# Graph network node update: both layers in one step, and a last update of 384 columns

## The chip, the core and the metric

The kernel runs on one core of a Trainium2 chip. The metric is the device time of one execution, in microseconds (us), as the median of several runs. The engines of the core are named as the profile names them: PE is TensorE (PEld its weight loads), DVE is VectorE, ACT is ScalarE, POOL is GpSimd, and SP issues most of the transfers.

## What is computed

There are 12500 nodes with 64 features and 200000 edges with 32 features; edges are sorted by destination. Each edge makes a message, messages are summed at the destination, and the node is updated, added to itself and normalized:

```python
msg_in = jnp.concatenate([nodes[row], nodes[col], edge_features], axis=-1)
messages = _mlp(msg_in, mW1, mb1, mW2, mb2)          # relu(x @ W1 + b1) @ W2 + b2
aggregated = jax.ops.segment_sum(messages, col, num_segments=nodes.shape[0])
upd_in = jnp.concatenate([nodes, aggregated], axis=-1)
x = _layernorm(x + _mlp(upd_in, uW1, ub1, uW2, ub2), axis=-1)
```

`row` is the source, `col` the destination. The hidden layers have 128 features.

## The kernel before

The product with the source's features is made once per node: a table A (L414 to L422) holds x @ W1 for the source part, a table B (L424 to L430) that for the destination part with the bias. Per edge, only rows of these tables are added.

The edges are cut into 1563 tiles of 128. A step of the main loop (L583) deals with one subgroup of 6 tiles (NSUB = 261 subgroups, the last of 3 tiles); two subgroups make a group of 12. For each tile POOL gathers 128 rows of A by an indirect DMA (L168); the gathered rows of a subgroup are one buffer of a pool with 18 (ROWB). The first 10 subgroups gather rows of x instead. All gathers are issued by POOL in order, as far ahead as buffers allow (L585).

In step s the loop does this, in this order on each engine:

- `norm` of an update (L358): on DVE a reciprocal and the scaling of each block of 128 nodes.
- `windows(s + 2)` (L217): SP loads 32 rows of B per tile (L229).
- `node_part(s)` (L260): DVE adds the gathered rows to the products in PSUM (L276), ACT applies relu (L277); this gives h.
- `collect(s - 1)` (L287): PE adds h into the sums of the open update by a selection matrix (L302), and counts edges (L307). The products transpose the result: 128 features by up to 480 node columns.
- `close` (L318): when the last subgroup of an update has been collected, ACT copies sums and counts to SBUF (L321, L322).
- every second step `select`, `load` and `counts` (L187 to L215): the selection matrices of the next group.
- `edge_part(s + 1)` (L246): PE makes the edge and destination products of the next subgroup in PSUM (L256).
- `carry` (L310): the sums of nodes that lie in both updates go over to the next one (L315, L316).
- `update` (L333): the first layer of the node update on PE, 448 columns (L337, L338), and its relu on ACT (L339, tile hTu).
- `residual` (L341): the second layer plus x on PE, for 4 blocks of 128 nodes (L346, L347), the statistics on DVE (L351, L353) and the square root on ACT (L355).
- `columns` (L326): SP loads the columns of x for an update (L330).
- `store` (L368): SP writes a finished update (L370).

Updates are not evenly spaced. A destination number is drawn as a square, so later edges hold more nodes; `updates()` (L51) places 33 of them, the first after 47 subgroups and the last ones every 4. `due` (L575) gives the step in which an update's first layer runs. Update 31 is due in step 258 and update 32, the last, in step 262; the loop runs to step 264. In the version before, the first layer runs in step `due` behind `edge_part`, the second layer in the step after it, norm and store in the one after that:

```python
            if s + 1 < NSUB:
                edge_part(s + 1)
            if s in due and due[s] + 1 < K:
                carry(due[s] + 1)
            if s in due:
                update(due[s])
            if s - 1 in due:
                residual(due[s - 1])
```

The order is written out by hand (manual_schedule): each engine runs its instructions in the order of these calls. The PSUM tiles pc (products), pu (first layer) and py (second layer) share two buffers; a new tile takes the one that was released first, and waits for its last reader.

After the loop a flag is read (L623); a branch for unusual inputs (L625) is not taken.

Of the kernel before, what the change touches and what calls it, by code (L numbers as in the profile page):

```python
# [10 lines left out]
F32 = mybir.dt.float32  # L11
I32 = mybir.dt.int32
AF = mybir.ActivationFunctionType
ALU = mybir.AluOpType
# [3 lines left out]
P = 128  # L18
N, D, DE, DH = 12500, 64, 32, 128
E = 200000  # L20
# [4 lines left out]
SUB = 6  # L25
# [5 lines left out]
WIN = 32  # L31
# [12 lines left out]
UB = 4  # L44
NCOL = (-(-N // P) + UB) * P
UN = 448
UW = UN + WIN
ONE = D - 1


def updates():  # L51


    def node(s):
        return N * min(1.0, s * SUB * P / E) ** 2
    at = [0]
    for s in range(1, NSUB):
        if s > at[-1] and node(s + 1) - node(at[-1]) > UN - WIN:
            at.append(s)
    return at  # L60


UPD = updates()


@with_exitstack
def gnn_kernel(ctx: ExitStack, tc: tile.TileContext, x1T, x, eT, e_rows, src, dst, dst_row, wrow, wnext, whalf,
# [24 lines left out]
    nc = tc.nc  # L92
    const = ctx.enter_context(tc.tile_pool(name="const", bufs=1))
    dram = ctx.enter_context(tc.tile_pool(name="dram", bufs=1, space=bass.MemoryType.DRAM))
    psum = ctx.enter_context(tc.tile_pool(name="psum", bufs=2, space=bass.MemoryType.PSUM))
# [5 lines left out]
    K = len(UPD)  # L101
# [9 lines left out]
    sums_s = [const.tile([P, UW], F32, name=f"sums_s{k}") for k in range(2)]  # L111
    xw = [const.tile([P, UB * P], F32, name=f"xw{k}") for k in range(2)]
    hT = const.tile([DH, UB * P], F32, name="hTu")
# [6 lines left out]
    uz = const.tile([P, DH], F32, name="uz")  # L120
    ub1_s = const.tile([DH, 1], F32, name="ub1_s")
    u2 = const.tile([DH, D], F32, name="u2")
    ux = const.tile([P, D], F32, name="ux")
    w2u = const.tile([DH, DH], F32, name="w2u")
    ident = const.tile([P, P], F32, name="ident")
    eps = const.tile([P, 1], F32, name="eps")
# [46 lines left out]
    with tc.tile_pool(name="sup", bufs=2) as sup, tc.tile_pool(name="work", bufs=2) as work, tc.manual_schedule():  # L173
# [136 lines left out]
        def carry(u):  # L310

            d = nc.values_load(ustep[0:1, u:u + 1], engines=[ET.PE], min_val=0, max_val=UW - WIN,
                               skip_runtime_bounds_check_because="they are limited to this")
            ps, pn = sums[u]
            nc.tensor.matmul(ps[:, :WIN], ident, sums_s[(u - 1) % 2][:, bass.ds(d, WIN)], start=False, stop=False)  # L315
            nc.tensor.matmul(pn[:, :WIN], ident[:, 0:1], xw[(u - 1) % 2][:, bass.ds(d, WIN)], start=False, stop=False)  # L316
# [6 lines left out]

        us = {}

        def columns(u):  # L326

            n0 = nc.values_load(usup[0:1, u:u + 1], engines=[ET.SP], min_val=0, max_val=N - 1,
                                skip_runtime_bounds_check_because="destinations are node numbers")
            nc.sync.dma_start(xw[u % 2][ONE:, :UN], x1T[:, bass.ds(n0, UN)])  # L330
            us[u] = n0

        def update(u):  # L333

            n0 = us[u]
            pu = psum.tile([DH, UN], F32, name="pu", tag="pc")
            nc.tensor.matmul(pu, w2u, sums_s[u % 2][:, :UN], start=True, stop=False)  # L337
            nc.tensor.matmul(pu, uz, xw[u % 2][:, :UN], start=False, stop=True)  # L338
            nc.scalar.activation(hT[:, :UN], pu, AF.Relu, bias=ub1_s)  # L339

        def residual(u):  # L341

            n0 = us[u]
            py = psum.tile([P, UB, D], F32, name="py", tag="pc")
            for i in range(UB):
                nc.tensor.matmul(py[:, i], xw[u % 2][:, i * P:(i + 1) * P], ux, start=True, stop=False)  # L346
                nc.tensor.matmul(py[:, i], hT[:, i * P:(i + 1) * P], u2, start=False, stop=True)  # L347
            st = work.tile([P, UB, nc.vector.BN_STATS_DIM], F32, name="st")
            mv = work.tile([P, UB, nc.vector.BN_AGGR_DIM], F32, name="mv")
            for i in range(UB):  # L350
                nc.vector.bn_stats(out=st[:, i], in_=py[:, i])  # L351
            for i in range(UB):
                nc.vector.bn_aggr(out=mv[:, i], in_=st[:, i])  # L353
            sd = work.tile([P, UB], F32, name="sd")
            nc.scalar.activation(sd, mv[:, :, 1], AF.Sqrt, bias=eps)  # L355
            us[u] = (n0, py, mv, sd)

        def norm(u):  # L358
            n0, py, mv, sd = us[u]
            rs = work.tile([P, UB], F32, name="rs")  # L360
            nc.vector.reciprocal(rs, sd)
            o = work.tile([P, UB, D], F32, name="o")
            for i in range(UB):
                nc.vector.tensor_scalar(o[:, i], py[:, i], mv[:, i, 0:1], rs[:, i:i + 1],
                                        op0=ALU.subtract, op1=ALU.mult)
            us[u] = (n0, o)

        def store(u):  # L368
            n0, o = us.pop(u)
            nc.sync.dma_start(out[bass.ds(n0, UB * P), :].rearrange("(c p) d -> p c d", p=P), o)  # L370


        WCH = 1024
# [50 lines left out]
        def chunk_b(c, into):  # L424
            pb, tb = products(c, w1b)
            n = min(NCH, NB - c)
            pf, tf = (t.rearrange("p h i f -> p (h i) f")[:, :n] for t in (pb, tb))
            nc.vector.tensor_tensor(tf, pf, b1.unsqueeze(1).broadcast_to([P, n, DH]), op=ALU.add)
            for v in into:
                nc.sync.dma_start(v[:, c:c + n, :], tf)  # L430
# [112 lines left out]
        def checks():  # L543

            mm = work.tile([P, 4], F32, name="mm", bufs=1)
            r = E - (NT - 1) * P

            nc.vector.tensor_reduce(mm[:, 0:1], drc, AX.X, ALU.max)
            nc.vector.tensor_reduce(mm[:, 1:2], drc[:, :NT - 1], AX.X, ALU.min)
            nc.vector.tensor_tensor(mm[:r, 1:2], mm[:r, 1:2], drc[:r, NT - 1:], op=ALU.min)  # L550

            back = work.tile([SUP, NSUP], F32, name="back", bufs=1)
            nc.vector.tensor_tensor(back, wb, wa, op=ALU.is_lt)
            nc.vector.memset(mm[:, 2:3], 0.0)
            nc.vector.tensor_reduce(mm[:SUP, 2:3], back, AX.X, ALU.add)
            nc.vector.tensor_scalar(mm[:, 0:1], mm[:, 0:1], float(WIN - 1), None, op0=ALU.is_gt)
            nc.vector.tensor_scalar(mm[:, 1:2], mm[:, 1:2], 0.0, None, op0=ALU.is_lt)
            nc.vector.tensor_reduce(mm[:, 3:4], mm[:, 0:3], AX.X, ALU.add)
            pf = psum.tile([1, 1], F32, name="pf", tag="pc")
            nc.tensor.matmul(pf, mm[:, 3:4], ones, start=True, stop=True)  # L560

            uf = work.tile([1, K + 1], F32, name="uf", bufs=1)
            nc.vector.tensor_copy(uf[:, :K], usup)
            nc.vector.memset(uf[:, K:], float(N))
            gap = work.tile([1, K + 1], F32, name="gap", bufs=1)
            nc.vector.tensor_tensor(gap[:, :K], uf[:, 1:], uf[:, :-1], op=ALU.subtract)
            nc.vector.tensor_scalar(gap[:, :K], gap[:, :K], float(UN), None, op0=ALU.is_gt)
            nc.vector.tensor_copy(gap[:, K:], past)
            bad = work.tile([1, 1], F32, name="bad", bufs=1)
            nc.vector.tensor_reduce(bad, gap, AX.X, ALU.add)  # L570
            nc.vector.tensor_tensor(flag_i, pf, bad, op=ALU.add)
# [3 lines left out]
        due = {(UPD[u + 1] if u + 1 < K else NSUB) + 1: u for u in range(K)}  # L575
# [4 lines left out]
        edge_part(0)  # L580
        gathered = XG
        chunks = list(range(NCH, NB, NCH))
        for s in range(last + 3):  # L583
            g, j = divmod(s, SUP // SUB)
            while gathered < NSUB and frees(gathered) < s:  # L585
                gather(gathered)
                gathered += 1
            if s - 2 in due:
                norm(due[s - 2])
            if s + 2 < NSUB:  # L590
                windows(s + 2)
            if s < NSUB:
                node_part(s)
            if 1 <= s <= NSUB:
                collect(s - 1)
            if s + 1 in due:
                close(due[s + 1])
            if j == 0 and g + 1 < NSUP:
                select(g + 1)
                load(g + 1)  # L600
                counts(g + 1)
            if j == 1 and g + 2 < NSUP:
                loadd(g + 2)
            if chunks and s >= BS and chunks[0] < NCH + NB * (s + 1 - BS) / (SUP // SUB * (GE - 1) - BS):
                chunk_b(chunks.pop(0), [Bv])
            if s + 1 < NSUB:
                if s + 1 < XG:
                    transpose(s + 1)
                edge_part(s + 1)
            if s in due and due[s] + 1 < K:  # L610
                carry(due[s] + 1)
            if s in due:
                update(due[s])
            if s - 1 in due:
                residual(due[s - 1])
            if s + 2 in due:
                columns(due[s + 2])
            rest(s)
            if s - 2 in due:
                store(due[s - 2])  # L620


    flag = nc.values_load(flag_i[0:1, 0:1], min_val=0, max_val=2 * EBULK,  # L623
# [163 lines left out]
```

## Time and profile before

| what | us |
|---|---|
| median of 3 runs | 1979.92 (1979.69 to 1980.9) |
| the profiled execution | 1980.06 |
| its span | 1978.3 |
| PE busy | 1520.7 (77%) |
| DVE busy | 554.1 (28%) |
| ACT busy | 359.1 (18%) |
| POOL busy | 1476.7 (75%) |

The span runs from the first to the last instruction of the program that was profiled. A row of the page's fifth part names a line, an engine, an operation and its tiles (out<-in) with their shapes; then come the count, the busy time in all, the mean of one in ns, and after a second bar the idle time of the engine just before these instructions with what ended most of it ("issue": nothing that the profile shows). A row of the timeline has the start, the time taken, the engine, the line, the operation, the count of merged instructions, and in brackets the idle time before it and what ended it. A row of the windows view has a stretch of the span, the busy time of PE, PEld, DVE, ACT and POOL in it, the granted TensorE clock as a share of full speed, the share of the DMA engines and GB/s. A float32 matmul appears as two passes.

### The profile page before, as it was taken

Reading aid. Unit: us, or ns where it says so; the run is one execution under the profiler, and the core shown is the slowest. Engines: PE = TensorE matmul, PEld = TensorE weight load, DVE = VectorE, ACT = ScalarE, POOL = GpSimd, SP = SyncE. Lnnn points to the kernel's source line nnn. Section 1 sums busy time; section 2 is a strip of 40 time slices with the busy share of each in tenths; the row PEclk is TensorE's granted clock in tenths of the full one; section 3 lists DMA queues with packets and bytes.
Section 4 is the critical chain, followed back from the end, with each engine's and each line's share of the span. In section 5 each row is a group of like instructions: output and inputs, shape, how many; then the busy total and the mean of one; then the engine's idle time right before and its main releaser. Section 6 shows DMA issues by size and latency. Waiting matters only on the chain.

```text
span 1978.3 us, 34854 instructions
## 1 busy us (share of the span) xinstructions
PE 1520.7 (77%) x9218; PEld 1321.6 (67%) x9218; DVE 554.1 (28%) x1165; ACT 359.1 (18%) x550; POOL 1476.7 (75%) x1572
## 2 busy tenths in 40 slices
PE   3796898876757676776777777778778888888987
PEld 2696787765656665666666666667666777777766
DVE  1423333322222322222222232222222323323322
ACT  0221111211111111111111111111112112122121
POOL 7777777777777777777777777777777777777774
PEclk8655555555555555555555555555555555555555
DMA  8634454433333333333333333333333333333332
GB/s 207 181 97 120 130 134 126 115 103 92 98 94 95 94 98 98 94 96 99 96 98 96 101 92 100 101 97 99 100 99 98 99 103 97 101 102 100 101 103 63
DMA packets 244063, 208.45 MB, mean 105 GB/s; under 512 B 78233, under 2 KB 208370, under 8 KB 243875
## 3 DMA queue, kind: packets, MB, share of 16 engines
q0 software_dynamic: 50016, 100.57, 20.3%
q1 hardware_dynamic: 179312, 96.69, 17.8%
q10 hardware_dynamic: 14546, 8.93, 1.6%
q8 instruction: 88, 1.44, 0.3%
q14 instruction: 101, 0.82, 0.1%
HBM read 188.25 MB, written 17.69 MB: 104 GB/s over the span
## 4 chain that ended last, share of the span: by engine, by line
POOL 53%; issue 28%; PE 9%; DMA 7%; DVE 1%; SPq 1%; ACT 0%; ACTq 0%; DVEq 0%; POOLq 0%
POOL xg L168 53%; PE sums L302 4%; DMA xg<-tab_a,src_s 4%; PE pc L256 3%; DMA tab_a<-tb 1%; PE pb L410 1%; DMA l<-in_eT 1%; DMA w1b<-in_mW 1%; SPq L229 1%; PE pc L270 1%; PE pt L236 0%; PE cnt L307 0%; DMA rhs<-tab_b 0%; DMA xall<-in_x1T 0%; DVE tb L418 0%
## 5 line engine op out<-in xcount | busy, mean ns | idle before, releaser
L168 POOL DMA_INDIRECT xg<-tab_a,src_s x1503 | 1418.5, 944 | 460.5 <-issue 449.8
L302 PEld LDWEIGHTS sums<-sel,h 128*128 128x128 f32 x3126 | 669.6, 320 | 365.3 <-ACT h L277 316.4
L302 PE MATMUL sums<-sel,h 128*128 128x32 f32 x3126 | 689.5, 391 | 278.7 <-ACT h L277 265.9
L276 DVE TENSOR_TENSOR h<-pc,xg 128x768 f32<-128x768 f32 x252 | 239.5, 951 | 1043.7 <-DMA xg<-tab_a,src_s 812.8
L256 PE MATMUL pc<-rhs,l 64*128 64x128 f32 x3126 | 444.2, 439 | 95.4 <-DVE h L276 54.2
L256 PEld LDWEIGHTS pc<-rhs,l 64*128 64x128 f32 x3126 | 366.6, 318 | 120.2 <-DVE h L276 58.0
L277 ACT ACTIVATE h<-h 128x768 f32<-128x768 f32 x252 | 211.2, 839 | 1116.6 <-DVE h L276 1055.0
L196 DVE TENSOR_TENSOR l<-l,cps 128x768 f32<-128x768 int32 (+1 forms) x134 | 127.8, 954 | 98.5 <-DMA l<-in_dst_row 94.8
L208 ACT CAST selb<-sel 128x384 bf16<-128x384 f32 x131 | 66.7, 509 | 181.0 <-DVE sel L200 167.7
L346 PE MATMUL py<-ux,xw 128*128 128x64 f32 x264 | 84.5, 423 | 1.6 <-DVE h L276 1.6
L307 PE MATMUL cnt<-selb,one 128*1 128x32 bf16 x1563 | 85.3, 189 | 0.0
L347 PE MATMUL py<-u,hTu 128*128 128x64 f32 x264 | 82.9, 417 | 0.4 <-ACT hTu L339 0.4
L337 PE MATMUL pu<-sums_s,w2u 128*128 128x448 f32 x66 | 61.4, 1034 | 22.3 <-DVE h L276 21.6
L200 DVE TENSOR_TENSOR sel<-cps,drc 128x384 f32<-128x384 f32 x131 | 71.8, 548 | 20.0 <-PE sums L302 19.9
L346 PEld LDWEIGHTS py<-ux,xw 128*128 128x128 f32 x264 | 69.9, 324 | 9.5 <-issue 7.6
L347 PEld LDWEIGHTS py<-u,hTu 128*128 128x128 f32 x264 | 71.2, 329 | 0.6 <-ACT hTu L339 0.6
L168 POOL DMA_INDIRECT xg<-in_x,src_s x60 | 57.1, 952 | 19.1 <-issue 18.0
L307 PEld LDWEIGHTS <-one 128*1 128x1 bf16 x1563 | 54.3, 83 | 23.0 <-issue 8.7
L351 DVE BATCH_NORM_STATS2 st<-py 128x6 f32<-128x64 f32 x132 | 20.6, 218 | 160.6 <-PE py L347 157.0
L338 PE MATMUL pu<-xw,uz 128*128 128x448 f32 x66 | 55.2, 940 | 0.0
L410 PE MATMUL pb<-w1a,xall 64*128 64x128 f32 x196 | 23.5, 411 | 33.7 <-DVE tb L418 22.2
L410 PEld LDWEIGHTS pb<-w1a,xall 64*128 64x128 f32 x196 | 21.4, 306 | 35.4 <-DVE tb L418 23.5
(87 smaller groups left out, 437.6 us busy)
## 6 DMA issues: line engine op xcount, KB each, us to landing
l<-in_dst_row SPq DMA_DIRECT2D x262, 96.0 KB
l<-in_eT SPq DMA_DIRECT2D x262, 96.0 KB
rhs<-tab_b SPq DMA_DIRECT2D x1563, 16.0 KB
xg<-tab_a,src_s POOLq DMA_INDIRECT x1503
tab_b<-tb SPq DMA_DIRECT2D x13, 512.0 KB
tab_a<-tb ACTq DMA_DIRECT2D x12, 512.0 KB
out<-o SPq DMA_DIRECT2D x33, 128.0 KB
xw<-in_x1T SPq DMA_DIRECT2D x33, 113.8 KB
```

Source lines behind the costliest of these rows:

```text
L168: nc.gpsimd.indirect_dma_start(out=a[:, i, :] if s < XG else a[:, i // 2, i % 2, :], out_offset=None, in_=A[:, :] if s >= XG else x[:, :], ...
L196: nc.vector.tensor_tensor(l[r], l[r].bitcast(I32), node[r].unsqueeze(2).broadcast_to([r.stop - r.start, SUP // 2, P]), op=ALU.is_equal)
L200: nc.vector.tensor_tensor(s[:, :nt], slot.unsqueeze(1).broadcast_to([P, nt, WIN]), drc[:, g * SUP:g * SUP + nt].unsqueeze(2).broadcast_to( ...
L208: nc.scalar.copy(sb[:, :nt], S[g][:, :nt])
L256: nc.tensor.matmul(pc[:, b, k, :], L[g][q:q + 64, m, :], rhs[g % 2][q:q + 64, m, :], start=s >= XG or k == 0, stop=s >= XG)
L276: nc.vector.tensor_tensor(h[:, b, :m], pc[:, b, :m], a[:, b, :m], op=ALU.add)
L277: nc.scalar.activation(h[:, b, :m], h[:, b, :m], AF.Relu)
L302: nc.tensor.matmul(ps[:, bass.ds(ws[i], WIN)], h[:, i % 2, i // 2, :], S[g][:, k0 + i, :], start=False, stop=ends and i == n - 1)
L307: nc.tensor.matmul(pn[:, bass.ds(ws[i], WIN)], one, SB[g][:, k0 + i, :], start=False, stop=ends and i == n - 1)
L346: nc.tensor.matmul(py[:, i], xw[u % 2][:, i * P:(i + 1) * P], ux, start=True, stop=False)
L347: nc.tensor.matmul(py[:, i], hT[:, i * P:(i + 1) * P], u2, start=False, stop=True)
L410: nc.tensor.matmul(pb[:, h, i, :], xl[64 * h:64 * h + 64, i * P:(i + 1) * P], w[64 * h:64 * h + 64], start=True, stop=True)
```

## The change

Carry and the first layer stand ahead of the next subgroup's products, and the second layer behind them in the same step; so norm and store come one step earlier, and the loop has one step less. The last update has UL = 384 columns and three blocks instead of 448 and four; the check on the gap between updates knows this width. Shortened to what matters:

```diff
+UL = min(UB, -(-int(N * (1 - (UPD[-1] * SUB * P / E) ** 2) + WIN) // P)) * P
...
+        def width(u):
+
+            return UN if u + 1 < K else UL
+
+        def blocks(u):
+            return UB if u + 1 < K else UL // P
...
-            nc.sync.dma_start(xw[u % 2][ONE:, :UN], x1T[:, bass.ds(n0, UN)])
+            nc.sync.dma_start(xw[u % 2][ONE:, :width(u)], x1T[:, bass.ds(n0, width(u))])
...
-            nc.tensor.matmul(pu, w2u, sums_s[u % 2][:, :UN], start=True, stop=False)
-            nc.tensor.matmul(pu, uz, xw[u % 2][:, :UN], start=False, stop=True)
-            nc.scalar.activation(hT[:, :UN], pu, AF.Relu, bias=ub1_s)
+            n = width(u)
+            pu = psum.tile([DH, UN], F32, name="pu", tag="pc")[:, :n]
+            nc.tensor.matmul(pu, w2u, sums_s[u % 2][:, :n], start=True, stop=False)
+            nc.tensor.matmul(pu, uz, xw[u % 2][:, :n], start=False, stop=True)
+            nc.scalar.activation(hT[:, :n], pu, AF.Relu, bias=ub1_s)
...
-            for i in range(UB):
+            for i in range(blocks(u)):
                 nc.tensor.matmul(py[:, i], xw[u % 2][:, i * P:(i + 1) * P], ux, start=True, stop=False)
                 nc.tensor.matmul(py[:, i], hT[:, i * P:(i + 1) * P], u2, start=False, stop=True)
...
-            nc.sync.dma_start(out[bass.ds(n0, UB * P), :].rearrange("(c p) d -> p c d", p=P), o)
+            nc.sync.dma_start(out[bass.ds(n0, blocks(u) * P), :].rearrange("(c p) d -> p c d", p=P), o[:, :blocks(u)])
...
-            nc.vector.tensor_scalar(gap[:, :K], gap[:, :K], float(UN), None, op0=ALU.is_gt)
+            nc.vector.tensor_scalar(gap[:, :K - 1], gap[:, :K - 1], float(UN), None, op0=ALU.is_gt)
+            nc.vector.tensor_scalar(gap[:, K - 1:K], gap[:, K - 1:K], float(min(UN, UL)), None, op0=ALU.is_gt)
...
-        for s in range(last + 3):
+        for s in range(last + 2):
...
-            if s - 2 in due:
-                norm(due[s - 2])
+            if s - 1 in due:
+                norm(due[s - 1])
...
+            if s in due and due[s] + 1 < K:
+                carry(due[s] + 1)
+            if s in due:
+                update(due[s])
             if s + 1 < NSUB:
                 if s + 1 < XG:
                     transpose(s + 1)
                 edge_part(s + 1)
-            if s in due and due[s] + 1 < K:
-                carry(due[s] + 1)
             if s in due:
-                update(due[s])
-            if s - 1 in due:
-                residual(due[s - 1])
+                residual(due[s])
             if s + 2 in due:
                 columns(due[s + 2])
             rest(s)
-            if s - 2 in due:
-                store(due[s - 2])
+            if s - 1 in due:
+                store(due[s - 1])
```

The loops over blocks of the statistics, the square root and norm are cut to `blocks(u)` in the same way.

More of the change, by code (lines that the diff above doesn't have):

```diff
@@ L329, in columns @@
                                 skip_runtime_bounds_check_because="destinations are node numbers")
-            nc.sync.dma_start(xw[u % 2][ONE:, :UN], x1T[:, bass.ds(n0, UN)])
+            nc.sync.dma_start(xw[u % 2][ONE:, :width(u)], x1T[:, bass.ds(n0, width(u))])
             us[u] = n0
         def update(u):
[L335 to L339, printed above, removed]
+            n = width(u)
[3 more added lines that the diff above has]
+            nc.scalar.activation(hT[:, :n], pu, AF.Relu, bias=ub1_s)
         def residual(u):
@@ L349, in residual @@
             mv = work.tile([P, UB, nc.vector.BN_AGGR_DIM], F32, name="mv")
-            for i in range(UB):
+            for i in range(blocks(u)):
                 nc.vector.bn_stats(out=st[:, i], in_=py[:, i])
-            for i in range(UB):
+            for i in range(blocks(u)):
                 nc.vector.bn_aggr(out=mv[:, i], in_=st[:, i])
             sd = work.tile([P, UB], F32, name="sd")
-            nc.scalar.activation(sd, mv[:, :, 1], AF.Sqrt, bias=eps)
+            nc.scalar.activation(sd[:, :blocks(u)], mv[:, :blocks(u), 1], AF.Sqrt, bias=eps)
             us[u] = (n0, py, mv, sd)
@@ L360, in norm @@
             rs = work.tile([P, UB], F32, name="rs")
-            nc.vector.reciprocal(rs, sd)
+            nc.vector.reciprocal(rs[:, :blocks(u)], sd[:, :blocks(u)])
             o = work.tile([P, UB, D], F32, name="o")
-            for i in range(UB):
+            for i in range(blocks(u)):
                 nc.vector.tensor_scalar(o[:, i], py[:, i], mv[:, i, 0:1], rs[:, i:i + 1],
```

## Prediction

> **What bounds the kernel now.** I read the page first, for the engine that never stops.
>
> ```profile
> span 1978.3 us, 34854 instructions
> ...
> POOL 53%; issue 28%; PE 9%; DMA 7%; DVE 1%; SPq 1%; ACT 0%; ACTq 0%; DVEq 0%; POOLq 0%
> ...
> L168 POOL DMA_INDIRECT xg<-tab_a,src_s x1503 | 1418.5, 944 | 460.5 <-issue 449.8
> L276 DVE TENSOR_TENSOR h<-pc,xg 128x768 f32<-128x768 f32 x252 | 239.5, 951 | 1043.7 <-DMA xg<-tab_a,src_s 812.8
> ```
>
> POOL's indirect gathers hold the chain. They wait for no buffer: nearly all of their idle time is issue, 449.8 us over 1503, or 0.30 us each. 0.94 busy and 0.30 issue make 1.25 us, and the first gather at 2.83 us, the last at 1956.04 and 1562 steps between them give the same 1.25. The adder of h (L276) waits 812.8 us for gathered rows, so TensorE, VectorE and ScalarE run behind POOL. A change on those three moves nothing before 1956.04. What it can move is the 22.3 us after that, read from the timeline (start, us, engine line).
>
> ```profile
> 1945.63 1.65 PE L256 MATMUL pc<-rhs,l 64*128 64x128 f32 x12
> 1948.62 1.86 PE L337 MATMUL pu<-sums_s,w2u 128*128 128x448 f32 x2 [0.59 <-DVE h L276]
> 1955.08 0.96 DVE L276 TENSOR_TENSOR h<-pc,xg 128x768 f32<-128x768 f32 x1 [5.22 <-DMA xg<-tab_a,src_s]
> 1956.04 0.94 POOL L168 DMA_INDIRECT xg<-tab_a,src_s  x1 [0.30 <-issue]
> 1956.09 0.69 PE L346 MATMUL py<-ux,xw 128*128 128x64 f32 x2 [1.59 <-DVE h L276]
> 1959.56 2.71 PE L302 MATMUL sums<-sel,h 128*128 128x32 f32 x12
> 1961.29 1.10 DVE L364 TENSOR_SCALAR o<-py,mv,rs 128x64 f32<-128x64 f32 x4
> 1962.30 0.61 DVE L276 TENSOR_TENSOR h<-pc,xg 128x256 f32<-128x256 f32 x2
> 1963.30 1.49 PE L302 MATMUL sums<-sel,h 128*128 128x32 f32 x6 [0.77 <-ACT h L277]
> 1965.44 1.86 PE L337 MATMUL pu<-sums_s,w2u 128*128 128x448 f32 x2 [0.48 <-ACT sums_s L321]
> 1968.83 0.63 ACT L339 ACTIVATE hTu<-pu,ub_s 128x448 f32<-128x448 f32 x1 [3.00 <-PE pu L338]
> 1972.90 1.10 DVE L364 TENSOR_SCALAR o<-py,mv,rs 128x64 f32<-128x64 f32 x4
> ```
>
> The second layer of update 31 (L346, L347) starts at 1956.09, when h of subgroup 259 has freed its PSUM buffer. It pushes the sums of 259 to 1959.56. Its norm ends at 1962.39 and stands on VectorE ahead of the last h (1962.30, while its rows were asked for at 1956.04). Then comes update 32 alone, with all it does on the path. The windows view, cut at the 3.41 us stretches in which the clock changes, gives TensorE's rate (first column after the stretch: PE busy; PEclk third from the end).
>
> ```profile
> 1949.23:1952.65 3.42, 3.42 (x9) 1.89 (x8) 0.63 (x2) 1.12 (x3) 2.50 (x4) 0.50 0.41 101
> 1952.65:1956.06 3.41, 1.85 (x21) 1.56 (x20) 0.96 (x1) 0.00 (x0) 2.50 (x4) 1.00 0.34 95
> 1956.06:1959.47 3.41, 3.38 (x16) 3.38 (x17) 0.00 (x0) 0.84 (x1) 0.92 (x1) 0.50 0.16 38
> 1959.47:1962.89 3.42, 3.06 (x20) 2.86 (x19) 2.69 (x15) 0.35 (x2) 0.00 (x0) 0.50 0.00 0
> 1966.30:1969.71 3.41, 3.00 (x7) 1.53 (x6) 0.00 (x0) 0.63 (x1) 0.00 (x0) 0.50 0.00 0
> 1969.71:1973.13 3.42, 1.67 (x14) 1.53 (x14) 1.31 (x10) 0.30 (x1) 0.00 (x0) 1.00 0.03 5
> ```
>
> Half clock is the rule; single stretches have the full one.
>
> **The change, part by part.** In mid-run an ordinary step costs TensorE 2.7 (12 sums passes) + 0.3 (counts) + 1.6 (L256) = 4.6 us of the 7.5 that six gathers take. An update adds opening the sums 0.9, carry 0.65, first layer 3.15, second layer 3.5. Before, these fall in two steps; after, in one, about 12 us. TensorE is then 4.5 us late, and the next two ordinary steps give it back (2.9 each). Updates are at least four steps apart: 4 x 4.6 + 8.2 = 26.6 us of 30. What hides it is the 18 gather buffers, so POOL would notice only a lag of many steps. Cost taken: 0. If that cover were gone, up to 4.5 us per update, 33 times.
>
> The wait is moved, not removed. The order of the instructions and their semaphores in the two programs show: before, the first layer waits for h of its own step (0.59 us above); after, it takes the older PSUM buffer and waits for h one step back, while the next L256 products, now behind it, wait for h of their own step. The second layer then waits for hTu. Its moved instructions are 16 passes on TensorE, 8 statistics and 5 norm instructions on VectorE, one square root on ScalarE, and on SP the store. The store now stands a step earlier, ahead of six row loads (L229) and waits for norm; SP's next loads serve products two steps off, 15 us, and need 3.1 us to issue. Taken: 0; at worst the few us of one step, hidden by the same buffers. At the end no row load is behind it, only the last columns (L330). They go out at about 1958 instead of 1951, and are needed in the first layer after 1963: about 3 us of room after a landing of some 2 us (estimated from the gathers' 2.66).
>
> *Order at the end, step 258, at half clock.* Carry can start when its register is there (read at 1945.35, offset written at 1945.77): 1945.85 instead of 1947.21. Carry 0.65 and first layer 0.16 + 4 x 0.75: TensorE is free at 1949.75, result 1949.96. L256 follows (h of 258 ended 1948.57): 1951.33. hTu: ScalarE is busy with selb to 1950.22, so 1950.25 + 0.63 = 1950.88, in time. Second layer 3.5 (16 x 0.214): last result 1955.03. From there to the end of norm before took 1962.39 - 1959.77 = 2.6: 1957.65. Behind norm on VectorE stands h of 259, its rows there since 1954.95: 1958.6, which is 2.6 later than before. Its relu 0.85: 1959.45. TensorE has done the sums of 258 by then; L256 of 260 waits for norm and is done at 1958.5. Sums of 259: 2.65 + 0.35: 1962.5. Sums of 260: 1.5: 1964.0. Before: 1964.8. So the order brings 0.8 us: the last h is no longer late, but h of 259 is.
>
> *The clock.* The Trainium skill (TensorE: Matmul & The Clock Gate, What's actually happening) says that a busy stretch of some 3.4 us opens the full clock. The trace agrees on the length but not on what counts as busy: 1956.06 to 1959.47 is 3.38 of 3.41 us busy and 0.50 follows; 1966.30 to 1969.71 is 3.00 busy and 1.00 follows. The latter holds the wide first layer. Set against the granted clock's record, each of the 17 full stretches after 352 us follows one in which L337 and L338 issue for 2.15 us or more; narrow passes never did it there. By the rule, TensorE would be at full clock from 1949.2 to the end: the sums of 260 would end near 1961, update 32 would be 1.6 us shorter still, and the gain with the width below would be about 7 us. By the rows one stretch follows the first layer, if it sits well in the grid: here 2.5 us of it would fall before 1949.23. The full stretch to 1952.65 then holds L256 and the second layer: last result about 1953.1, norm 1955.7, h of 259 1956.6, sums of 260 1962.0: a gain of 2.8. Before, the same kind of stretch covers sums of 258 and L256, which then wait anyway. I follow the rows. How the grid lies differs from run to run, so both ends, 0.8 and 2.8, occur; as the first layer has 2.2 of its 3.0 us in one stretch in somewhat over half of all positions, I take 1.8.
>
> *Width 384.* First layer: 4 passes x 0.75 x 64/448 = 0.43. hTu 0.63 x 64/448 = 0.09. One block less in the second layer: 4 passes at 0.11 (full clock, as here) 0.45, at half 0.85. VectorE: a quarter of 0.62 + 0.29 + 1.10 = 0.5. Store 96 instead of 128 KB: nothing to 0.3, taken 0.1. Sum 1.55 to 1.95. Against it: a first layer of 2.56 us opens a full stretch less often; if the second layer then runs at half clock, 10 passes lose 1.0. I take 1.5, with ends 0.5 and 2.0. The extra compare on VectorE in mid-run lies beside gathers: 0.
>
> Sum: 1.8 + 1.5 = 3.3. The profiled execution has 1980.06, span 1978.3 and 1.76 around it: 1976.8. The median of the runs lies 0.14 under that execution: 1979.92 - 3.3 = 1976.6.
>
> **Rivals.** *A, the likeliest*: as summed, 1976.6, own range 1975.2 to 1978.2. *B*: the full stretch falls on the second layer of 31 and again on that of 32. Then 2.8 + 2.0 = 4.8: 1975.1. For it: the position in this trace would do the first. Against: both need a good place. *C*: order brings nothing, since h of 259 stands behind norm; only the width counts: 1978.4. For it: the 2.6 us by which h of 259 is later. Against: even at half clock 0.8 is left. *D, slower*: VectorE's queue at step 259. Norm of 31 stands before h of 259, and from norm's end to the end of the sums it is 6.35 us; with 1.5 from the width the tail breaks even when norm ends at 1959.9, and is 4 us slower at 1963.9. That needs TensorE to enter step 258 some 6 us late, with the debt of update 30 (step 254) unpaid: 1984. Against: in this trace TensorE waits for relu at 1942.27, and after has 26.6 of 30 us. *That the change doesn't do what it says*: the program has 384 columns and three blocks in the last update, so the width is real; that the products stand between the layers is, too.
>
> **Numbers.** 0.2% is 3.96 us, about what a measurement of this kernel can tell from no change: 1975.96 to 1983.88. A 0.60, of which 0.09 lies below 1975.96; B 0.22; C 0.12; D 0.06. Faster 0.31, same 0.63, slower 0.06. Range 1974.8 to 1979.0: B's middle and C are in; some of B and all of D, under 2 in 10, are out.
>
> **What would show it.** Last gather still at 1956.0, with issue as its only wait. First layer of 31 at about 1946.6; its second layer 1951 to 1953-1955; norm before h of 259, which starts at 1955.6 to 1957.6; sums of 260 ending 1962 to 1964; from their end to the end of the span 12 us instead of 13.5. It is wrong if a gather waits for a buffer, if columns (L330) or carry's register come late, or if norm ends after 1958.

## Result and profile after

The changed kernel takes 1977.51 us (median of 17 runs, 1975.47 to 1979.66), the kernel before 1980.09 us in the runs beside it (17 runs, 1977.68 to 1982.42). The ratio is 0.9984, with a 95% interval of 0.9978 to 0.9991: 0.16% faster, within 0.2%. The prediction had 1976.6 us and a range of 1974.8 to 1979.0. The page of the changed kernel, whose lines have moved by 2 to 10:

```profile
span 1976.1 us, 34864 instructions
...
POOL 47%; issue 25%; PE 8%; DMA 5%; DVE 1%; ACT 1%; SPq 0%; DVEq 0%; POOLq 0%; ACTq 0%
...
L170 POOL DMA_INDIRECT xg<-tab_a,src_s x1503 | 1418.2, 944 | 461.0 <-issue 448.8
L278 DVE TENSOR_TENSOR h<-pc,xg 128x768 f32<-128x768 f32 x252 | 239.7, 951 | 1100.8 <-DMA xg<-tab_a,src_s 937.7
...
L355 PE MATMUL py<-ux,xw 128*128 128x64 f32 x262 | 56.8, 302 | 18.9 <-ACT hTu L348 18.9
```

POOL is as it was: 448.8 us of issue, no wait for a buffer. VectorE waits longer for gathered rows (937.7 us against 812.8), so the other engines have more room than before. New is the mean of a second-layer pass: 302 ns, where the page of before has this row:

```profile
L346 PE MATMUL py<-ux,xw 128*128 128x64 f32 x264 | 84.5, 423 | 1.6 <-DVE h L276 1.6
```

The timeline of the end:

```profile
1946.23 1.86 PE L346 MATMUL pu<-sums_s,w2u 128*128 128x448 f32 x2
1949.52 1.65 PE L258 MATMUL pc<-rhs,l 64*128 64x128 f32 x12
1951.52 0.43 PE L355 MATMUL py<-ux,xw 128*128 128x64 f32 x2 [0.36 <-ACT hTu L348]
1955.04 1.10 DVE L373 TENSOR_SCALAR o<-py,mv,rs 128x64 f32<-128x64 f32 x4
1956.05 0.95 DVE L278 TENSOR_TENSOR h<-pc,xg 128x768 f32<-128x768 f32 x1
1956.21 0.94 POOL L170 DMA_INDIRECT xg<-tab_a,src_s  x1 [0.30 <-issue]
1958.30 2.77 PE L304 MATMUL sums<-sel,h 128*128 128x32 f32 x12 [0.89 <-ACT h L279]
1959.74 0.62 DVE L278 TENSOR_TENSOR h<-pc,xg 128x256 f32<-128x256 f32 x2 [2.73 <-DMA xg<-tab_a,src_s]
1961.26 1.49 PE L304 MATMUL sums<-sel,h 128*128 128x32 f32 x6
1962.79 0.56 ACT L323 COPY sums_s<-sums 128x480 f32<-128x480 f32 x1 [1.92 <-PE sums L304]
1963.40 1.65 PE L346 MATMUL pu<-sums_s,w2u 128*128 128x384 f32 x2 [0.48 <-ACT sums_s L323]
1966.36 0.58 ACT L348 ACTIVATE hTu<-pu,ub_s 128x384 f32<-128x384 f32 x1 [2.58 <-PE pu L347]
1970.71 0.85 DVE L373 TENSOR_SCALAR o<-py,mv,rs 128x64 f32<-128x64 f32 x3
```

The second layer of update 31 now runs from 1951.52, ahead of h of subgroup 259. The last h starts at 1959.74, when its rows are there, and not behind a norm; the last sums start at 1961.26 instead of 1963.30. The sums of 259 now wait for relu, since h of 259 stands behind norm and starts at 1956.05 instead of 1955.08. The clock in the windows view of the changed kernel:

```profile
1950.98:1954.39 3.41, 3.05 (x28) 2.87 (x26) 0.83 (x8) 0.49 (x1) 2.57 (x3) 0.99 0.36 117
...
1964.64:1968.05 3.41, 3.06 (x10) 2.07 (x9) 0.00 (x0) 0.58 (x1) 0.00 (x0) 0.50 0.00 0
1968.05:1971.46 3.41, 1.34 (x7) 1.15 (x6) 1.63 (x10) 0.30 (x1) 0.00 (x0) 0.50 0.02 5
```

The second layer of 31 has the full clock, that of update 32 has half. Before it was the other way round.

### The profile page after: what moved, and what is told of

Read it like the earlier page. It is cut to its first block, busy times and chain, and to the rows that moved or that the text cites. A ratio compares the mean times of both kernels' runs of the same rounds, so it can differ in the third digit from the quotient of the medians.

```text
span 1976.1 us, 34864 instructions
## 1 busy us (share of the span) xinstructions
PE 1435.5 (73%) x9214; PEld 1228.2 (62%) x9214; DVE 554.2 (28%) x1163; ACT 356.6 (18%) x550; POOL 1476.3 (75%) x1572
## 4 chain that ended last, share of the span: by engine, by line
POOL 47%; issue 25%; PE 8%; DMA 5%; DVE 1%; ACT 1%; SPq 0%; DVEq 0%; POOLq 0%; ACTq 0%
POOL xg L170 47%; DMA xg<-tab_a,src_s 4%; PE sums L304 2%; PE pc L258 1%; PE pu L346 1%; PE pu L347 1%; DMA l<-in_eT 1%; PE py L355 1%; PE py L356 1%; DVE h L278 1%; ACT h L279 0%; PE pb L419 0%; PE sums L317 0%; DVE st L360 0%; DMA l<-in_dst_row 0%
## 5 line engine op out<-in xcount | busy, mean ns | idle before, releaser
L170 POOL DMA_INDIRECT xg<-tab_a,src_s x1503 | 1418.2, 944 | 461.0 <-issue 448.8
L304 PE MATMUL sums<-sel,h 128*128 128x32 f32 x3126 | 676.2, 385 | 403.5 <-ACT h L279 392.5
L304 PEld LDWEIGHTS sums<-sel,h 128*128 128x128 f32 x3126 | 644.1, 311 | 472.9 <-ACT h L279 450.3
L278 DVE TENSOR_TENSOR h<-pc,xg 128x768 f32<-128x768 f32 x252 | 239.7, 951 | 1100.8 <-DMA xg<-tab_a,src_s 937.7
L258 PE MATMUL pc<-rhs,l 64*128 64x128 f32 x3126 | 420.1, 424 | 55.4 <-DVE o L373 27.0
L258 PEld LDWEIGHTS pc<-rhs,l 64*128 64x128 f32 x3126 | 346.3, 306 | 113.5 <-DVE o L373 30.1
L355 PE MATMUL py<-ux,xw 128*128 128x64 f32 x262 | 56.8, 302 | 18.9 <-ACT hTu L348 18.9
L346 PE MATMUL pu<-sums_s,w2u 128*128 128x448 f32 (+1 forms) x66 | 61.2, 1032 | 0.5 <-ACT sums_s L323 0.5
L355 PEld LDWEIGHTS py<-ux,xw 128*128 128x128 f32 x262 | 44.1, 211 | 25.8 <-ACT hTu L348 23.6
L360 DVE BATCH_NORM_STATS2 st<-py 128x6 f32<-128x64 f32 x131 | 20.5, 219 | 129.2 <-PE py L356 129.2
L356 PE MATMUL py<-u,hTu 128*128 128x64 f32 x262 | 55.5, 297 | 0.3 <-ACT hTu L348 0.3
L347 PE MATMUL pu<-xw,uz 128*128 128x448 f32 (+1 forms) x66 | 51.7, 882 | 0.0
L356 PEld LDWEIGHTS py<-u,hTu 128*128 128x128 f32 x262 | 44.3, 212 | 0.5 <-ACT hTu L348 0.5
```

The source lines that it names most:

```text
L170: nc.gpsimd.indirect_dma_start(out=a[:, i, :] if s < XG else a[:, i // 2, i % 2, :], out_offset=None, in_=A[:, :] if s >= XG else x[:, :], ...
L258: nc.tensor.matmul(pc[:, b, k, :], L[g][q:q + 64, m, :], rhs[g % 2][q:q + 64, m, :], start=s >= XG or k == 0, stop=s >= XG)
L278: nc.vector.tensor_tensor(h[:, b, :m], pc[:, b, :m], a[:, b, :m], op=ALU.add)
L304: nc.tensor.matmul(ps[:, bass.ds(ws[i], WIN)], h[:, i % 2, i // 2, :], S[g][:, k0 + i, :], start=False, stop=ends and i == n - 1)
L346: nc.tensor.matmul(pu, w2u, sums_s[u % 2][:, :n], start=True, stop=False)
L347: nc.tensor.matmul(pu, uz, xw[u % 2][:, :n], start=False, stop=True)
```

## Experiments

The theory: the change acts only between the last gather and the end of the span, by the order (TensorE and VectorE late at the end) and by the width of update 32. Rivals: only one of the two counts; or the crowded step costs POOL time in mid-run. When the last gather is issued differs from run to run by reasons that have nothing to do with the change (1954.1 to 1959.4 in the twelve profiles of kernels with 18 buffers; the first gathers of table A come up to 4.0 us behind the one before them, and the pitch is 1.2484 or 1.2508 us). So the profiles are compared from the last gather on: to the start of the copy of the last sums on ScalarE (which ends what the order can move; it starts at 1962.79 above, and in the kernel before at 1964.83), and from there to the end of the span (which the width can shorten). The last column is the clock of the second layer of update 31 and of update 32.

| profile | to the sums, us | sums to end, us | clock 31, 32 |
|---|---|---|---|
| before | 8.79 | 13.46 | half, full |
| changed | 6.58 | 13.27 | full, half |
| order only | 6.66 | 14.85 | full, half |
| width only | 8.56 | 12.59 | half, full |
| norm later | 6.26 | 12.31 | full, full |
| 256 columns | 6.80 | 11.33 | full, half |
| before without layer 31 | 5.45 | 14.74 | none, half |
| changed without layer 31 | 5.46 | 12.80 | none, half |
| changed again | 8.80 | 12.46 | half, full |
| norm later again | 6.98 | 13.24 | mostly half, half |
| wide fill | 6.34 | 12.16 | full, full |
| narrow fill | 6.97 | 12.23 | full, full |

The runs of one kernel spread over 3 to 5 us, so beside the ratios I give the difference of the means of all runs of a kernel and of the kernel before on the same chip, with the standard error worked out from those runs.

**One part alone.** Order only: the last update keeps its width.

```diff
-UL = min(UB, -(-int(N * (1 - (UPD[-1] * SUB * P / E) ** 2) + WIN) // P)) * P
+UL = UN
...
-            return UB if u + 1 < K else UL // P
+            return UB
```

> The new order with the last update still 448 columns wide. Tail theory (both parts of the change work after the last gather, and nowhere else): about 1.8 us faster than before (0.8 to 2.8, as the full clock falls), with the sums of the last subgroup ending near 1962.8 instead of 1964.8 in the profile. Rival (only the width counts, since h of subgroup 259 now stands behind norm): no difference, sums ending at 1964.8.

Width only: the loop of before, with the new `width` and `blocks` (norm and store go back a step too).

```diff
+            if s + 1 < NSUB:
...
+                edge_part(s + 1)
             if s in due and due[s] + 1 < K:
                 carry(due[s] + 1)
             if s in due:
                 update(due[s])
-            if s + 1 < NSUB:
...
-                edge_part(s + 1)
-            if s in due:
-                residual(due[s])
+            if s - 1 in due:
+                residual(due[s - 1])
```

> The order of before with the last update 384 columns wide. Tail theory: 0.5 to 2.0 us faster than before; the stretch from the end of the last sums to the end of the span goes from 13.5 us to 12 us where the last second layer has the full clock, and to 13.3 us where it has half. Rival (only the width counts): 2.6 us faster. Rival (only the order counts): 0.

Measured: order only 1977.09 us against 1979.13, ratio 0.9990 (0.9981 to 0.9999), means -2.2 us with a standard error of 0.5. Width only 1978.22, ratio 0.9994 (0.9985 to 1.0003), means -1.2 with 0.4. The ratio of width only includes no change; its mean and the table speak for a gain. The timeline of width only has the stall of before:

```profile
1957.03 0.69 PE L355 MATMUL py<-ux,xw 128*128 128x64 f32 x2 [1.83 <-DVE h L278]
...
1962.22 1.10 DVE L373 TENSOR_SCALAR o<-py,mv,rs 128x64 f32<-128x64 f32 x4
...
1963.24 0.61 DVE L278 TENSOR_TENSOR h<-pc,xg 128x256 f32<-128x256 f32 x2
```

The last gather of this run was issued at 1957.21, so the last h starts 6.0 us after it; before 6.3, in the changed kernel 3.5. The order moves the first column of the table by about 2 us and not the second; the width moves the second and not the first. Both rivals of the kind "only one counts" fall.

**The second layer of update 31 left out.** In both orders its products, statistics, norm and store are not issued, so those nodes are not written. In the order of before:

```diff
-            if s - 1 in due:
+            if s - 1 in due and due[s - 1] != K - 2:
                 residual(due[s - 1])
```

> The kernel before without the second layer, norm and store of update 31, whose 384 or so nodes are not written. Tail theory: the second layer of 31 is what keeps the sums of 259 and the last h back, so without it the sums of 260 end near 1961.7 (landing of the last rows at 1959.7 + 0.4 + 0.4 + 1.3) instead of 1964.8: about 3 us faster than before. Rival (it lies beside the last gathers): no difference.

> The changed kernel without the second layer, norm and store of update 31. Tail theory: the sums of 260 end near 1961.7 to 1962 as in the kernel before without them, 0.8 to 1 us earlier than in the changed kernel; what is left of the time is that of before without them, less the width's 0.5 to 2 us. Rival (the new order is late for another reason, such as carry ahead of the products): as late as the changed kernel, 1962.8.

Measured: kernel before without it 1976.38 us against 1979.22, ratio 0.9985 (0.9976 to 0.9994); changed without it 1974.47, ratio 0.9977 (0.9968 to 0.9986). In the first:

```profile
1957.28 0.62 DVE L276 TENSOR_TENSOR h<-pc,xg 128x256 f32<-128x256 f32 x2 [3.24 <-DMA xg<-tab_a,src_s]
...
1958.20 1.49 PE L302 MATMUL sums<-sel,h 128*128 128x32 f32 x6 [0.20 <-ACT h L277]
```

The last h waits for its rows alone, 3.0 us after the last gather (1954.28). Without this layer both orders reach the sums at the same 5.45 us. The mean of the kernel before falls by 3.0 us, as expected. So, with one profile of each, the layer is all that makes the two orders differ: set against the profiles of the full kernels it cost 3.3 us before the sums in the order of before, and still costs 1.1 in the new one (0.8 to 1 expected). Carry ahead of the products shows no cost.

**Norm behind the last h.** Norm and store of update 31 alone are put a step later, behind the additions of the last subgroup.

```diff
-            if s - 1 in due:
+            if s - 1 in due and due[s - 1] != K - 2:
                 norm(due[s - 1])
...
                 node_part(s)
+            if s - 2 in due and due[s - 2] == K - 2:
+                norm(due[s - 2])
```

> The changed kernel, but norm and store of update 31 stand behind the last h instead of ahead of h of subgroup 259. Tail theory: h of 259 starts when its rows have landed (about 1955.1 instead of 1956.05), the sums of 259 no longer wait for its relu, but those of 260 are then held by the landing of the last rows (h at 1959.7 in the changed kernel's trace), so the sums end near 1962.3: 0.4 to 0.5 us faster than the changed kernel. Rival (VectorE's queue is not what is late): the same as the changed kernel.

> Norm and store of update 31 behind the last h, once more, beside the changed kernel. Tail theory: 0.5 to 1.4 us faster than the changed kernel (0.3 to 0.5 from the earlier sums, seen in the profiles, and up to 1.0 from the clock of the last second layer, which differs from run to run); rival (the 1.4 us between the earlier medians was chance): no difference in the mean.

> The changed kernel once more, on the same chip as the next run. Tail theory: 2 to 3.3 us faster than before; from the last gather to the end of the span 19 to 20.5 us, as the clock of the last second layer falls.

Measured: first 1975.17 against 1979.13, ratio 0.9980 (0.9971 to 0.9989). In that profile h of 259 starts as soon as its rows have landed, ahead of the last gather:

```profile
1955.15 0.96 DVE L278 TENSOR_TENSOR h<-pc,xg 128x768 f32<-128x768 f32 x1
...
1956.24 0.94 POOL L170 DMA_INDIRECT xg<-tab_a,src_s  x1 [0.30 <-issue]
```

The sums come 0.3 us sooner than in the first profile of the changed kernel (0.4 to 0.5 expected); the other 1.0 us by which the stretch after the last gather is shorter is the clock of update 32. Beside each other, on another chip: 1981.30, 1982.52 for the changed kernel and 1984.11 for before, both ratios 0.9987 (0.9978 to 0.9996). Means on that chip: -2.4 with 0.5 for the changed kernel, -2.9 with 0.5 for norm later. The profile of the changed kernel there shows what half clock does to the new order:

```profile
1952.06 0.96 DVE L278 TENSOR_TENSOR h<-pc,xg 128x768 f32<-128x768 f32 x1 [7.61 <-DMA xg<-tab_a,src_s]
...
1954.57 0.63 ACT L348 ACTIVATE hTu<-pu,ub_s 128x448 f32<-128x448 f32 x1
...
1955.26 0.69 PE L355 MATMUL py<-ux,xw 128*128 128x64 f32 x2 [1.25 <-ACT hTu L348]
...
1959.39 0.95 POOL L170 DMA_INDIRECT xg<-tab_a,src_s  x1 [0.30 <-issue]
...
1960.45 1.10 DVE L373 TENSOR_SCALAR o<-py,mv,rs 128x64 f32<-128x64 f32 x4
...
1961.47 0.95 DVE L278 TENSOR_TENSOR h<-pc,xg 128x768 f32<-128x768 f32 x1
```

One product of the second layer follows the other after 0.43 us instead of 0.22, norm ends at 1961.55, and h of 259 starts 2.1 us after the last gather; in the other profile of the changed kernel 0.2 before it, in norm later 1.1 before it. The sums come at 8.80 us: the order has gained nothing in this run. From the last gather to the end it takes 21.3 us, outside the 19 to 20.5 expected. The full clock was not missing; it came too soon:

```profile
1951.60:1955.01 3.41, 1.63 (x14) 0.75 (x12) 2.21 (x4) 1.46 (x3) 2.52 (x3) 1.00 0.21 55
1955.01:1958.43 3.42, 3.17 (x15) 3.18 (x16) 0.00 (x0) 0.19 (x1) 2.50 (x4) 0.50 0.35 101
```

The rows of subgroup 258 were late, so its h (1952.06), the work behind it on ScalarE and with it hTu (1954.57) were late too. The second layer began 0.25 us after the full stretch had ended. Norm later keeps h of 259 on time in either clock, but in its second profile, mostly at half clock, the sums come at 6.98, since TensorE itself is late with the sums of 258. It has the lower median in each place where all nodes are written and no filler is added; that it is faster than the changed kernel is not settled by these runs (-0.5 us in the means, with a standard error of 0.7, on the one chip where they ran side by side).

**Width once more.** `UL = 256`; the last 70 or so nodes are not written, and the check on the gap keeps its old bound.

```diff
-UL = min(UB, -(-int(N * (1 - (UPD[-1] * SUB * P / E) ** 2) + WIN) // P)) * P
+UL = 256
```

> The changed kernel with a last update of 256 columns, so the last 70 or so nodes are not written. It takes the width's cost once more. Tail theory: another 0.4 (first layer) + 0.1 (hTu) + 0.45 or 0.85 (second layer) + 0.4 (statistics and norm) = 1.3 to 1.8 us faster than the changed kernel, where the clock of the last second layer is the same; a first layer of 1.7 us can no longer open a full stretch (it needed 2.15 us), so the last second layer is always at half clock. Rival (width is worth nothing): 0.

Measured 1974.73 against 1979.13, ratio 0.9978 (0.9969 to 0.9987). From the sums to the end 11.33 us: 1.9 less than the 13.27 and 13.24 with 384 columns at half clock, a little more than the 1.8 of the upper end (1.5 less than the 12.80 of the run without layer 31).

**Two gather buffers.** The rows of table A get a pool of their own with two buffers.

```diff
-ROWB = 18
+NR = 2
...
-    rows = ctx.enter_context(tc.tile_pool(name="rows", bufs=ROWB))
+    rows = ctx.enter_context(tc.tile_pool(name="rows", bufs=(XG + 1) // 2))
+    rows2 = ctx.enter_context(tc.tile_pool(name="rows2", bufs=NR))
...
```

> The kernel before with two buffers instead of 18 for the rows gathered from table A. From the start of a subgroup's gathers the rows two subgroups back must have been added, which leaves POOL about 3.8 us of slack a subgroup (7.5 less 2.7 landing and 1.0 adding). Cover theory (18 buffers hide the crowded step): the order of before is late by 1 to 1.4 us in each of two steps and stays within that slack, so at most some 10 us slower than before. Rival (an update costs POOL nothing in either order): the same as the changed kernel with two buffers.

> The changed kernel with two buffers for the rows gathered from table A. Cover theory: a step with an update takes TensorE 12 us for 7.5, so h of the next subgroup is 3 to 4.5 us late and POOL waits 0 to 2 us for its buffer 33 times: up to 60 us slower than the changed kernel, 20 to 40 us slower than the kernel before with two buffers. Rival (the crowded step is absorbed anyway): no slower than the kernel before with two buffers.

Measured: 2021.60 (ratio 1.0212, 1.0197 to 1.0228) and 2018.61 (1.0187, 1.0170 to 1.0204) against 1979.22. Both miss what I expected of them. Pitch by pitch, all of the extra time in POOL, 44.3 and 49.6 us, lies in the first 17 subgroups, where the others are still starting; from subgroup 45 on POOL waits 0.0 us in either order. So in mid-run two buffers are enough, and the crowded step doesn't reach POOL even then. What this experiment made slower is the start, not the updates.

**What opens the clock.** To norm later, eight bf16 products of 448 columns (wide) or seven float32 products of 32 columns with their weight loads (narrow), 3.0 us each at half clock, were added in 41 steps between 48 and 140; their PSUM tile was widened for it. The wide ones:

```diff
+            if 48 <= s < 140 and s % 2 == 0 and s not in due:
+                for _ in range(8):
+                    nc.tensor.matmul(cps[:, 64:], zero_b[:, :P], zero_b[:, :448], start=True, stop=True)
```

> The same with eight products of 448 columns and zeros added behind the edge products of 41 steps between step 48 and 140, 3.0 us each at half clock. Theory (wide products open the full clock, about 2.15 us of them in a stretch): some 20 to 35 more stretches at full clock between 360 and 1060 us of the span than without (13 of them without), and the same time, as TensorE runs behind POOL there. Rival (any busy stretch does it): the same as with narrow products.

> The same with seven float32 products of 32 columns in those places, each with its weight loads, 3.0 us at half clock too. Theory (wide products open the full clock): no more stretches at full clock between 360 and 1060 us than without, about 13, and the same time. Rival (any busy stretch does it): 20 to 35 more.

From 360 to 1060 us, the windows view of norm later (second run), wide and narrow:

```profile
360.00:1060.00 700.00, 483.57 (x3023) 419.95 (x3023) 180.35 (x340) 119.14 (x176) 529.14 (x561) 0.52 0.36 96
```

```profile
360.00:1060.00 700.00, 542.09 (x3348) 425.65 (x3347) 180.24 (x340) 119.05 (x176) 529.28 (x561) 0.58 0.36 97
```

```profile
360.00:1060.00 700.00, 584.92 (x3582) 529.98 (x3584) 179.83 (x340) 119.20 (x176) 529.20 (x561) 0.54 0.36 96
```

In the granted clock's record that is 34.1, 112.6 and 51.2 us at full clock, or 10, 33 and 15 stretches of 3.41 us (13 in the first run of norm later). Narrow products keep TensorE busier (584.9 us) than wide ones (542.1), yet they opened nothing by themselves: in that run all 8 openings between 360 and 1060 us follow the first layer of one of the 8 updates there, as in norm later, and 7 of them last two stretches (5 and 2 in the two runs of norm later). In the wide run there are 27 openings, of which 20 follow no first layer. The two fills differ in width, type and number of weight loads at once, so what counts besides the width is not separated. Times: 1979.98 (ratio 0.9981, 0.9972 to 0.9990) and 1980.01 (0.9979, 0.9970 to 0.9988) against 1984.11. 59 and 101 us more of TensorE's busy time in mid-run cost nothing. That both come out 1.3 us below norm later on that chip was not expected; the four profiles there differ by the clock at the end (first and last column of the table), and no more is shown.

## Why the prediction was right, point by point

The bound, the place of the gain and the two mechanisms are right. That the sum came near is in part luck: the order brought a little more than taken, the width a little less, and the misses partly cancel.

- **The bound.** Right. POOL waits for no buffer, the last gather is where it was, and everything that was gained lies behind it: 22.3 us from the last gather to the end before, 19.9 after.
- **Mid-run cost 0.** Right, but the reason was too cautious: from subgroup 45 on two buffers hide the crowded step as well as 18. "Up to 4.5 us per update" without that cover was not seen. The crowded step was also over-sized, since it was worked out at half clock: in the trace of the changed kernel 29 of the 33 second layers run mostly at full clock, in that of before 1.
- **The order, 1.8 us taken, 0.8 to 2.8.** The mechanism is right: pu at 1946.23 (1946.5 to 1946.6 worked), the last h on its rows, h of 259 behind norm. Its mean, 2.2 us, is near. The ends were mis-sized: in the profiles it gains 2.2 us with the full clock on layer 31 and 0.0 with half, where 2.8 and 0.8 were worked out. The lower end took the rows of 258 to be on time. In the run with half clock they were not (VectorE waits for them until 1952.06, 3.9 us after their last gather, against 3.4 in the first profile), and this, not a clock that stayed shut, put the second layer behind the full stretch.
- **The clock.** That the full clock falls on the second layer in "somewhat over half of all positions" was too low. In the records of the new order 30 to 33 of the 33 updates are followed by a full stretch (31 in the first profile of the changed kernel), and 25 to 30 second layers run mostly at full clock; in the order of before 15 to 21 updates are followed by one, and at most one second layer has it. The 2.15 us of first-layer products that the full stretches of the kernel before had ahead of them are no threshold: in the new order stretches with 1.1 to 1.4 us of them (counted at 0.75 us a pass at half clock) were followed by full clock too. There the products of 128 columns follow the first layer at once, and they seem to count with it; that this is the cause is argued from the order and from the fills, and not shown by a run of its own.
- **The width, 1.5 us taken, 0.5 to 2.0.** Measured 1.2 in the means. At equal clock from the sums to the end: 14.8 to 13.1 us at half (means of two and three profiles: -1.7, worked 1.95), 13.46 to 12.35 at full, the mean of five (-1.1, worked 1.55). First layer (3.39 to 2.96 us, to the start of hTu) and the way from the statistics to the store's issue (2.61 to 2.16) are as worked out. The term that was mis-sized is the store, "nothing to 0.3" less: from its issue to the end of the span it takes 4.15 to 4.27 us with 512 packets (four profiles), and 4.42 to 4.86 with 384 in eight profiles. A ninth has 4.00; it is the 12.80 of the table. Why the smaller store is no quicker stays open.
- **The sum.** The two parts alone give 3.45 us in the means, where 3.3 was summed; together 2.7 (standard error 0.4) and, on another chip, 2.4 (0.5). Whether the parts take something from each other, or this is chance, stays open. In the first profile of the changed kernel it is the clock: update 32 loses its full stretch and with it 0.9 us, so the second column falls by only 0.2. The prediction had this loss as "against it", at 1.0.
- **Rivals.** B (both full clocks) happened in the first profile of norm later and in those of the fills, not in those of the changed kernel. C (order brings nothing) is a single run, not the mean. D didn't come: norm ended at 1956.1, and even in the late run (2.2 us after the last gather, against the 3.9 worked out) the break-even was not passed.

## What to carry to other kernels

When one engine issues without a wait from the start to the end, only what lies behind its last instruction can be gained; look there for the in-order queue that holds finished work behind unfinished work. A layer can be moved ahead of the last input's arrival, but its DVE work then stands ahead of that input, and the TensorE clock decides whether this hurts: work out both clocks. Compare such small gains from the last instruction of the bounding engine on, since the start-up differs by more than the gain.

## What the hardware showed beside this

- A stretch of 3.41 us full of narrow passes (3.38 us busy) was followed by half clock. Of 27 openings between 360 and 1060 us in the run with 41 wide fills 20 follow no first layer; in the run with 41 narrow fills none of 8.
- A store of 384 packets of 256 bytes (96 KB) ended no sooner than one of 512: its last packet ended 1.50 to 2.21 us after issue in nine profiles, against 1.65 to 1.75 with 512 in four.
- The pitch of the indirect gathers is 1.2484 to 1.2487 us in most profiles and 1.2508 or 1.2509 in two, which is over 3 us in the run, more than the change.
